# V's projection one slot later, denominators by ones in the last step but one, and products with V in parts, in a conditioned attention kernel

## The chip, the cores and the metric

One core of a Trainium2 chip runs the whole program. The metric is the time of one execution in microseconds (us). The kernel before takes 739.61 us, the median of three runs (739.45 to 740.35). Engines: PE is TensorE (matrix products), with PEld its loading of weights; ACT is ScalarE, DVE is VectorE, POOL is GpSimd, SP is SyncE, which issues nearly all transfers.

## The reference

For each of 8 sequences of 512 tokens with 512 features: attention with 16 heads of 32, with the projection of one conditioning token added to Q and K, and the input added to the result.

```python
Q = _split_heads(x @ Wq.T + bq)
K = _split_heads(x @ Wk.T + bk)
V = _split_heads(x @ Wv.T + bv)
tQ = _split_heads(tokens @ Wq.T + bq)
tK = _split_heads(tokens @ Wk.T + bk)
cQ = Q + tQ
cK = K + tK
scores = jnp.einsum('bhqd,bhkd->bhqk', cQ, cK) / jnp.sqrt(jnp.float32(HEAD_DIM))
attn = jax.nn.softmax(scores, axis=-1)
out = jnp.einsum('bhqk,bhkd->bhqd', attn, V)
x = x + out.transpose(0, 2, 1, 3).reshape(B, S, D_MODEL)
```

All is fp32.

## The kernel before, in words

**Tiling.** The work is 32 steps t (`T = B * G`), one for each sequence and group of four heads: step t is sequence t // 4, group t % 4. Scores are computed twice. Once with queries on the partitions, 128 queries (`qc`) by 512 keys for each of the four heads: from these DVE takes the row maxima (`row_max`, lines 470 to 480) and ACT the denominators, as a sum that accompanies an exponential whose own output is thrown away (`denominators`, L521). And once with keys on the partitions, 128 keys (`kc`) by 512 queries: there PE first puts the negative maxima in every row (L563, a product of ones with the maxima split in three bf16 pieces), adds the scores (L566), and ACT writes the exponentials to SBUF (`exponentials`, L577). These are the moving side of the product with V (`times_v`, L582), four heads beside each other in the columns of the array. The four `kc` of a step are called its chunks; a score burst is four products, which the trace shows as eight records, since an fp32 product runs in two passes.

**Maxima.** When the four `qc` of a step have their maxima, POOL splits them (`split_max`, L535 to L538), PE transposes them (L547), and DVE or ACT copies them from PSUM (`transpose_max`, L553). The exponentials of that step need this copy.

**Projections.** Q, K and V of two groups (for V, of half a sequence) are computed by a product scheme of seven half-size products instead of eight, split in two halves, `first_products` and `other_products`; DVE puts the parts together (`plus`, L414 and L417, and L432 to L447). The blocks of combined weights are made by POOL (`combine_w`) and of combined inputs by DVE (`combine_x`).

**The loop.** For t from 0 to 28 a step has four quarters. Quarter i issues `exponentials(t, i)`, then a `row_max` of step t+1 (in the last quarter of step t+2), and then one piece of other work: a half of Q's projection, the product of step t-1 with V and its output (`weighted`), a half of K's, a half of V's. V's half in step t is number r = t % 4 of the next sequence, while Q's and K's are those of the slot before (`qk_of`, line 806). In the last quarter `transpose_max(t + 1)` is put into V's half.

**Banks.** PSUM is one tile of eight banks. `TURNS` is a table of bank orders, eight of them used in turn by the loop: entries 0 to 3 hold the quarter's exponentials, 4 to 7 its row scores, and the other work takes banks from entries 0 to 3 again, once ACT has read the exponentials. A quarter's banks must have been read by ACT and DVE before the next quarter writes them.

**Order.** The order on PE, ACT, DVE and POOL is that of the program, and each engine takes its instructions strictly in it. SP's transfers stand in the order of issue too. Waits are put in by the framework where tiles are shared.

**Prologue.** Lines 700 to 774: transposes of weights and of the first sequence, Q and K of the first two groups, then five bursts of row maxima, (0,0) to (0,3) and (1,0), each with its denominators, and between them halves of projections: Q's two, K's first, V's two.

**Outputs.** Through step 27 the product with V stays transposed: `weighted` (lines 606 to 637) makes the reciprocals of the denominators in that layout with a small product (L621), DVE turns 32x32 blocks (L632), POOL multiplies (L633) and adds the residual (L634), and four small transfers on SP store it (L637). The residual xr has three buffers; it is loaded by four small transfers and gets V's bias on POOL (L170). From step 28 on (`turned_by_vector`, line 152) another way is used: `untranspose` on PE, `divide` on DVE, `finish`, one large transfer each way (L166, L667).

**The end.** Steps 29 to 31 are written out by hand (lines 857 to 964). The projections are over, so the row maxima of step 31 are spread in half bursts over step 29 and 30 (`row_max_pair`, `row_max_pairs`), steps 28 and 29 take their product with V in two pieces, and `keep_busy` issues 22 products whose result nobody reads. Step 31 has no denominators on ACT: DVE adds exponentials (L922, L926), and products with ones (`times_ones`, L592) give the sums over the keys.

Of the kernel before, what the change touches and what calls it, by code (L numbers as in the profile page):

```python
# [17 lines left out]
def kernel(  # L18
# [65 lines left out]
        (6, 7, 2, 3, 0, 1, 4, 5),  # L84
        (7, 2, 0, 1, 3, 4, 5, 6),
        (3, 0, 1, 2, 6, 7, 4, 5),
        (6, 7, 0, 1, 4, 5, 2, 3),
        (4, 5, 0, 1, 6, 7, 2, 3),
        (6, 7, 0, 1, 4, 5, 2, 3),
        (4, 7, 0, 1, 2, 3, 5, 6),  # L90
        (0, 3, 1, 2, 6, 7, 4, 5),

        (6, 7, 4, 5, 2, 3, 0, 1),
        (6, 7, 2, 3, 0, 1, 4, 5),
        (6, 7, 0, 1, 4, 5, 2, 3),
        (6, 7, 4, 5, 2, 3, 0, 1),
        (6, 7, 2, 3, 4, 5, 0, 1),
# [52 lines left out]
    def turned_by_vector(t):  # L150

        return t < T - 4
# [317 lines left out]
    def row_max(t, qc):  # L470
        if t >= T:
            return
        open_max(t)
        for j in range(HG):
            row_scores(t, qc, j, banks(HG + j))
        for j in range(2):
            nc.vector.tensor_reduce(  # L477
                nmax[t][:, qc, j : j + 1, 0], banks(HG + j), AX.X, ALU.max, negate=True
            )
        row_max_of(t, qc, 1, banks(HG + 2, 2))  # L480
# [16 lines left out]
    def row_max_pair(t, qc, pr, at=2):  # L497

        open_max(t)
        for i in range(2):  # L500
            row_scores(t, qc, pr * 2 + i, banks(at + i))
        row_max_of(t, qc, pr, banks(at, 2))

    def row_max_pairs(t, of, late=()):

        open_max(t)
        for k, (qc, pr) in enumerate(of):
            for i in range(2):
                row_scores(t, qc, pr * 2 + i, banks(HG + k * 2 + i))
        row_max_of(t, *of[0], banks(HG, 2))  # L510
        for f in late:
            f()
        row_max_of(t, *of[1], banks(HG + 2, 2))

    def denominators(t, qc, prs=range(NP)):

        if t >= T - 1:
            return
# [71 lines left out]
    def times_ones(of, pt, start):  # L590
        for j in range(HG):
# [5 lines left out]
                stop=not start,  # L597
            )

    oT = {}  # L600

    def leave(t, pt):
        oT[t] = op.tile([P, S], F32, tag="oT", name=f"oT_{t}")
        nc.vector.tensor_copy(oT[t], pt)

    def weighted(t, pt, pd, between):


# [7 lines left out]
        )  # L616
        for kc in range(NS):
            times_v(t, kc, pt)
            if kc == 0:
                for h in range(HG):  # L620
                    nc.tensor.matmul(  # L621
                        pd[h * BL : (h + 1) * BL, : NB],
                        modulo,
                        apart[:, h].rearrange("p c a -> p (c a)"),
                        start=True,
                        stop=True,
                    )
        rec = op.tile([P, NB, 1], F32, tag="recs", name=f"recs_{t}")
        nc.vector.reciprocal(rec, pd[:, :NB].unsqueeze(2))
        between()  # L630
        y = op.tile([P, NB, BL], F32, tag="res", name=f"res_{t}")
        nc.vector.transpose(y.rearrange("p f e -> p (f e)"), pt)  # L632
# [11 lines left out]

    res = {}

    recs = {}

    def invert(t, den):
        recs[t] = op.tile([P, NS, HG, 1], F32, tag="rec", name=f"rec_{t}")  # L650
        nc.vector.reciprocal(recs[t], den)

    def divide(t, pt):
        res[t] = op.tile([P, NS, P], F32, tag="res", name=f"res_{t}")
        nc.vector.tensor_tensor(
            res[t].rearrange("p c (h e) -> p c h e", h=HG),
            pt.rearrange("p (c h e) -> p c h e", c=NS, h=HG),
            recs[t].broadcast_to([P, NS, HG, HD]),
            ALU.mult,
        )  # L660

    def finish(t):
        b, g = divmod(t, G)
        y = res.pop(t)
# [331 lines left out]
```

## Time and profile before

| What | Value |
|---|---|
| median of three runs | 739.61 us |
| the profiled execution: its own time | 740.33 us |
| its span, first to last instruction | 737.5 us |
| PE busy | 729.1 us |
| ACT busy | 626.4 us |
| DVE busy | 529.9 us |
| POOL busy | 166.2 us |
| L521, exponentials for the denominators | 496 of 701 ns, and 496 reads of the sum of 219 ns |
| L577, exponentials kept | 512 of 603 ns |
| L493, maxima of two heads | 132 of 1214 ns |
| additions of 128x512 on POOL (L634) | 28 of 1273 ns |
| large residual loads, issue to landing | 3.8 us |

The execution is inside the span by 2.8 us, which belong to the launch and its end. A row such as "L521 ... x496 | 338.0, 701" says: 496 instructions of line 521, 338.0 us busy in total, 701 ns on average. In a timeline a row has its start, its length, the engine, the line, the operation and its tiles; the brackets say how long the engine had been idle and what ended that.

### The profile page before, as it was taken

What the parts mean: (1) busy time and instruction counts of PE and PEld (TensorE: products, weight loads), DVE (VectorE), ACT (ScalarE), POOL (GpSimd) and SP (SyncE); (2) the same over time, 40 slices, a digit from 0 to 9 for tenths busy, and PEclk for the clock granted to TensorE, in tenths of its full rate; (3) what the DMA queues carried; (4) which work ended last, traced back from release to release, by engine and by line L of the source; (5) the groups of instructions that cost most, each with busy time, mean ns of one, the idle gap of its engine ahead of it and who ended that gap; (6) DMA issues with size and microseconds to landing.
All of it is one profiled execution on the core that took longest, in us unless ns stands there. A gap on an engine that the chain in (4) does not pass through costs nothing.

```text
span 737.5 us, 15136 instructions
## 1 busy us (share of the span) xinstructions
PE 729.1 (99%) x5434; PEld 406.9 (55%) x5434; DVE 529.9 (72%) x851; ACT 626.4 (85%) x1567; POOL 166.2 (23%) x270
## 2 busy tenths in 40 slices
PE   9999999999999999999999999999999999999997
PEld 6576555655555665555565555565555555555432
DVE  3589677777677776787866877777767777667764
ACT  2569889888898988988988988988989898898965
POOL 3721211222211222211122221122221122221130
PEclk9999999999999999999999999999999999999999
DMA  8512212122212222212222221212110111110111
GB/s 263 84 20 39 35 25 44 30 44 44 38 25 40 38 35 44 44 26 34 42 31 44 44 32 27 44 30 44 30 26 9 26 30 29 30 29 12 33 30 29
DMA packets 184766, 29.63 MB, mean 40 GB/s; under 512 B 178410, under 2 KB 182506, under 8 KB 184692
## 3 DMA queue, kind: packets, MB, share of 16 engines
q1 hardware_dynamic: 184112, 28.01, 22.1%
q8 instruction: 42, 0.69, 0.4%
q10 hardware_dynamic: 580, 0.68, 0.3%
q14 instruction: 32, 0.26, 0.1%
HBM read 20.27 MB, written 8.39 MB: 39 GB/s over the span
## 4 chain that ended last, share of the span: by engine, by line
PE 97%; DVE 1%; ACT 1%; DMA 0%; issue 0%; DVEq 0%
PE psum L394 26%; PE psum L582 16%; PE psum L484 15%; PE psum L566 15%; PE psum L391 14%; PE psum L563 6%; PE psum L338 2%; PE psum L547 1%; ACT e L577 1%; PE psum L254 1%; DMA x<-in_x_dram 0%; PE psum L299 0%; PE psum L641 0%; DVE nmax L477 0%; PE psum L592 0%; PE psum L680 0%
## 5 line engine op out<-in xcount | busy, mean ns | idle before, releaser
L521 ACT ACTIVATE dead<-psum,nmax 128x512 f32<-128x512 f32 x496 | 338.0, 701 | 8.3 <-DVE nmax L477 5.4
L577 ACT ACTIVATE e<-psum 128x512 f32<-128x512 f32 x512 | 264.3, 603 | 73.0 <-PE psum L566 72.9
L477 DVE TENSOR_REDUCE nmax<-psum 128x1 f32<-128x512 f32 x248 | 159.7, 686 | 149.5 <-PE psum L484 149.5
L493 DVE TENSOR_REDUCE nmax<-psum 128x2 f32<-128x1024 f32 x132 | 160.2, 1214 | 2.8 <-PE psum L484 2.8
L484 PE MATMUL psum<-kT,qT 32*128 32x512 f32 x1024 | 140.3, 602 | 0.2 <-DVE kT L417 0.2
L566 PE MATMUL psum<-qT,kT 32*128 32x512 f32 x1024 | 132.6, 588 | 0.0
L633 POOL TENSOR_TENSOR res<-res,recs 128x512 f32<-128x512 f32 x28 | 29.3, 1047 | 436.9 <-DVE res L632 436.9
L582 PE MATMUL psum<-e,v 128*32 128x512 f32 x1024 | 120.3, 596 | 1.0 <-ACT e L577 0.9
L521 ACT ACTIVATION_READ_ACCUMULATOR dead<-psum,nmax 128x1 f32 x496 | 108.6, 219 | 0.0
L484 PEld LDWEIGHTS psum<-kT,qT 32*128 32x128 f32 x1024 | 56.7, 183 | 61.0 <-ACT dead L521 26.8
L582 PEld LDWEIGHTS psum<-e,v 128*32 128x32 f32 x1024 | 26.8, 110 | 65.9 <-issue 41.1
L563 PE MATMUL psum<-maxT,onesb 3*128 3x512 bf16 x512 | 51.4, 384 | 1.5 <-DVE maxT L553 0.8
L566 PEld LDWEIGHTS psum<-qT,kT 32*128 32x128 f32 x1024 | 51.2, 185 | 2.5 <-issue 0.2
L391 PE MATMUL psum<-wc_v,xc 128*128 128x256 f32 x192 | 49.3, 379 | 0.0
L563 PEld LDWEIGHTS <-onesb 3*128 3x128 bf16 x512 | 13.3, 91 | 60.4 <-issue 50.9
L394 PE MATMUL psum<-xc,wc_q 128*128 128x256 f32 x180 | 46.2, 379 | 0.0
L394 PE MATMUL psum<-xc,wc_k 128*128 128x256 f32 x180 | 46.2, 379 | 0.0
L391 PEld LDWEIGHTS psum<-wc_v,xc 128*128 128x128 f32 x192 | 36.5, 190 | 5.0
L391 PE MATMUL psum<-wT_v,xT 128*128 128x256 f32 x128 | 38.7, 404 | 0.0
L394 PEld LDWEIGHTS psum<-xc,wc_q 128*128 128x128 f32 x180 | 34.2, 190 | 4.7
L394 PEld LDWEIGHTS psum<-xc,wc_k 128*128 128x128 f32 x180 | 34.2, 190 | 4.7
L634 POOL TENSOR_TENSOR res<-res,xr 128x512 f32<-128x512 f32 x28 | 35.7, 1273 | 2.2
(158 smaller groups left out, 776.2 us busy)
## 6 DMA issues: line engine op xcount, KB each, us to landing
x<-in_x_dram SPq DMA_DIRECT2D x112, 64.0 KB, 2.4
xr<-in_x_dram SPq DMA_DIRECT2D x112, 64.0 KB, 2.5
out_dram<-res SPq DMA_DIRECT2D x112, 64.0 KB, 2.0
w_q<-in_L_cond_Wq_dram SPq DMA_DIRECT2D x4, 256.0 KB, 4.5
w_k<-in_L_cond_Wk_dram SPq DMA_DIRECT2D x4, 256.0 KB, 4.3
w_v<-in_L_cond_Wv_dram SPq DMA_DIRECT2D x4, 256.0 KB, 5.1
xr<-in_x_dram SPq DMA_DIRECT2D x4, 256.0 KB, 3.8
out_dram<-res SPq DMA_DIRECT2D x3, 256.0 KB, 2.4
```

What stands on the lines that cost most here:

```text
L391: nc.tensor.matmul(pt, xb, w, start=(kc == kcs[0]), stop=(kc == kcs[-1]))
L394: nc.tensor.matmul(pt, w, xb, start=(kc == kcs[0]), stop=(kc == kcs[-1]))
L477: nc.vector.tensor_reduce(nmax[t][:, qc, j : j + 1, 0], banks(HG + j), AX.X, ALU.max, negate=True)
L484: nc.tensor.matmul(pt, qkT["q", t][r, qc * P : (qc + 1) * P], qkT["k", t][r, :], start=True, stop=True,)
L493: nc.vector.tensor_reduce(nmax[t][:, qc, pr * 2 : pr * 2 + 2, 0], pt, AX.X, ALU.max, negate=True)
L521: nc.scalar.activation(dead, banks(HG + j), AF.Exp, bias=nmax[t][:, qc, j, :], accum_out=sums[t][:, qc, j, :],)
L563: nc.tensor.matmul(bank[j], onesb[r, :], maxT[t][r, :], start=True, stop=False)
L566: nc.tensor.matmul(bank[j], qkT["k", t][r, kc * P : (kc + 1) * P], qkT["q", t][r, :], start=False, stop=True,)
L577: nc.scalar.activation(e[:, i, :], bank[pr * 2 + i], AF.Exp)
L582: nc.tensor.matmul(pt[j * HD : (j + 1) * HD, :], vs[b % 2][:, kc, (g * HG + j) * HD : (g * HG + j + 1) * HD], es[t, kc, j // 2][:, j % 2, ...
L633: nc.gpsimd.tensor_tensor(y, y, rec.broadcast_to([P, NB, BL]), ALU.mult)
L634: nc.gpsimd.tensor_tensor(y, y, xr.pop(t), ALU.add)
```

## The change

V's halves in the loop are now those of the same slot as Q's and K's, so one half leaves the prologue (where K's second half takes the place of V's), V of the first sequence is made during step 0, and step 28 still has one. All entries of `TURNS` for the loop and the three last steps are new; the five of the prologue are the same.

Step 30 has no denominators on ACT either; it gets them as step 31 does, by sums of exponentials on DVE and POOL and products with ones. The row maxima of steps 30 and 31 are taken in full bursts of four heads, in two instructions of two heads on DVE, to the last quarter of step 30, and the fillers are gone. Through step 30 the output goes the transposed way with small transfers. The products with V of steps 28 to 30 are made in parts of one or two chunks: ACT copies each part from PSUM and POOL adds it to the ones before.

```diff
@@ turned_by_vector / row_max / denominators @@
-        return t < T - 4
+        return t < T - 1
...
+        if t < T - 2:
+            for j in range(2):
+                nc.vector.tensor_reduce(
+                    nmax[t][:, qc, j : j + 1, 0], banks(HG + j), AX.X, ALU.max, negate=True
+                )
+        else:
+            row_max_of(t, qc, 0, banks(HG, 2))
         row_max_of(t, qc, 1, banks(HG + 2, 2))
...
-        if t >= T - 1:
+        if t >= T - 2:
             return
@@ prologue @@
     other_products("q", 0, 1, lambda: denominators(0, 2), nothing, (0, 1))
-    first_products("k", 0, 1, nothing, nothing, 3, 2)
     advance()
     row_max(0, 3)
     split_max(0)
-    first_products("v", 0, 0, lambda: denominators(0, 3), nothing, 2, 3)
+    first_products("k", 0, 1, lambda: denominators(0, 3), nothing, 2, 3)
...
-    other_products("v", 0, 0, lambda: denominators(1, 0), nothing, (0, 2))
+    other_products("k", 0, 1, lambda: denominators(1, 0), nothing, (0, 2))
@@ loop @@
-            other_products("k", 0, 1, dens, nothing, (0, 3))
+            first_products("v", 0, 0, dens, nothing, 3)
...
-            first_products("v", 0, 1, dens, nothing, 1)
-            combine_x(1, 0)
+            dens()
+            other_products("v", 0, 0, nothing, nothing, (1, 0))
...
-            other_products("v", 0, 1, dens, nothing, (0, 3))
+            first_products("v", 0, 1, dens, nothing, 3)
+            combine_x(1, 0)
...
-        project_pair("v", b + 1, r, dens, small, (0, 2) if r % 2 else 1)
+        project_pair("v", *of, dens, small, 1 if r % 2 else (0, 2))
@@ the parts @@
+    def part_of(t, pt, of, between=None):
+
+        for k, kc in enumerate(of):
+            if k and between:
+                between()
+            times_v(t, kc, pt, of)
+        if t in parts:
+            p = op.tile([P, S], F32, tag="dead", name=f"part_{t}_{of[0]}")
+            nc.scalar.copy(p, pt)
+            nc.gpsimd.tensor_tensor(parts[t], parts[t], p, ALU.add)
+        else:
...
+            nc.scalar.copy(parts[t], pt)
...
+    def send_parts(t, den):
+        rec = op.tile([P, NB, 1], F32, tag="recs", name=f"recs_{t}")
+        nc.vector.reciprocal(rec, den)
+        send(t, parts[t], rec)
@@ steps 29 to 31 @@
+    t = T - 3
...
+    row(3)
+    exponentials(t, 3)
+    row_max(t + 2, 0)
+    part_of(t, banks(0), [0, 1], lambda: transpose_max(t + 1, banks(1), nc.scalar.copy))
+    send_parts(t - 1, den)
+
+    t = T - 2
+    row(0)
+    exponentials(t, 0)
+    row_max(t + 1, 1)
+    apart = masked(t - 1)
+    part_of(t - 1, banks(0), [2])
+    load_residual(t + 1)
+    row(1)
+    exponentials(t, 1)
+    row_max(t + 1, 2)
+    part_of(t - 1, banks(0), [3])
+    spread_sums(apart, banks(1))
+    den = denominators_of(t - 1, banks(1))
+    row(2)
+    exponentials(t, 2)
+    row_max(t + 1, 3)
+    acc = room_for_sums(t)
+    sum_of(t, acc, 1, nc.gpsimd, [0])
+    split_max(t + 1)
+    part_of(t, banks(0), [0])
+    send_parts(t - 1, den)
+
+    exponentials(t, 3, (1, 2, 3, 4))
+    sum_of(t, acc, 1, nc.vector, [1])
+    part_of(
+        t, bank(5), [1, 2], lambda: transpose_max(t + 1, bank(0), nc.vector.tensor_copy)
+    )
+    sum_of(t, acc, 2, nc.vector)
+    sum_of(t, acc, 3, nc.vector)
+
+    t = T - 1
+    exponentials(t, 0, (6, 7, 1, 2))
+    part_of(t - 1, bank(3), [3])
+    exponentials(t, 1, (0, 4, 5, 6))
+    pv = bank(7)
+    times_v(t, 0, pv)
+    exponentials(t, 2, (1, 2, 3, 0))
+    times_v(t, 1, pv)
+    times_ones(acc, bank(4), True, True)
...
+    sum_of(t, acc2, 1, nc.vector)
...
+    send_parts(t - 1, den[:, :, 0:1])
+    exponentials(t, 3, (5, 6, 1, 2))
+    times_v(t, 2, pv)
+    pd = bank(3)
+    times_ones(acc2, pd, True, False)
+    times_ones([es[t, 2, pr] for pr in range(NP)], pd, False, False)
+    times_ones([es[t, 3, pr] for pr in range(NP)], pd, False, True)
+    times_v(t, 3, pv)
```

`sum_of(t, to, kc, on, prs)` adds exponentials of chunk `kc` to the sums, for pairs of heads `prs`, on the engine `on`; `room_for_sums` takes a tile for them; `masked`, `spread_sums` and `send` are pieces of the old `weighted`; `row(i)` sets the bank order. The loop's bank orders:

```diff
-        (6, 7, 2, 3, 0, 1, 4, 5),
-        (7, 2, 0, 1, 3, 4, 5, 6),
-        (3, 0, 1, 2, 6, 7, 4, 5),
-        (6, 7, 0, 1, 4, 5, 2, 3),
-        (4, 5, 0, 1, 6, 7, 2, 3),
-        (6, 7, 0, 1, 4, 5, 2, 3),
-        (4, 7, 0, 1, 2, 3, 5, 6),
-        (0, 3, 1, 2, 6, 7, 4, 5),
...
+        (3, 0, 1, 2, 4, 5, 6, 7),
+        (4, 5, 0, 1, 2, 3, 6, 7),
+        (2, 5, 0, 1, 3, 4, 6, 7),
+        (0, 5, 3, 4, 6, 7, 1, 2),
+        (6, 7, 4, 5, 0, 1, 2, 3),
+        (4, 5, 0, 1, 2, 3, 6, 7),
+        (2, 5, 0, 1, 6, 7, 3, 4),
+        (6, 7, 0, 1, 2, 3, 4, 5),
```

## The prediction

> **What bounds the kernel now.** First the totals of the page and its chain of work that ended last, then the busy times by stretch, then the timeline of a quarter of the loop with a store and the load behind it, of the prologue, and of the end.
>
> ```profile
> span 737.5 us, 15136 instructions
> PE 729.1 (99%) x5434; PEld 406.9 (55%) x5434; DVE 529.9 (72%) x851; ACT 626.4 (85%) x1567; POOL 166.2 (23%) x270
> ...
> PE 97%; DVE 1%; ACT 1%; DMA 0%; issue 0%; DVEq 0%
> ```
>
> TensorE carries 97% of the chain. A busy PE row hides short waits, so I read its pace from the starts of its bursts. By stretch:
>
> ```profile
> core 0: us, PE busy (x) PEld busy (x) DVE busy (x) ACT busy (x) POOL busy (x), PEclk, DMA share, GB/s
> 500.00:600.00 100.00, 100.00 (x756) 56.69 (x752) 74.74 (x121) 89.48 (x227) 23.88 (x40) 1.00 0.18 28
> 680.00:690.00 10.00, 9.13 (x76) 3.81 (x78) 6.62 (x10) 9.52 (x26) 2.19 (x5) 1.00 0.28 55
> 690.00:700.00 10.00, 9.31 (x94) 5.21 (x90) 8.05 (x11) 9.14 (x25) 1.27 (x1) 1.00 0.05 12
> 700.00:710.00 10.00, 9.01 (x80) 3.35 (x72) 7.30 (x9) 7.22 (x18) 3.41 (x6) 1.00 0.15 42
> ```
>
> In the loop PE never rests; from 680 us, where the projections have ended, ACT is the fuller engine (9.52 of 10 us) and PE waits. The timeline of one quarter of the loop (in step 28), in which step 27's output leaves:
>
> ```profile
> 676.25 0.39 PE L563 MATMUL psum<-maxT,onesb 3*128 3x512 bf16 x4
> 677.24 1.05 POOL L633 TENSOR_TENSOR res<-res,recs 128x512 f32<-128x512 f32 x1 [15.56 <-DVE res L632]
> 677.34 1.02 PE L484 MATMUL psum<-kT,qT 32*128 32x512 f32 x8
> 677.53 2.06 ACT L577 ACTIVATE e<-psum 128x512 f32<-128x512 f32 x4 [0.86 <-PE psum L566]
> 678.36 1.27 POOL L634 TENSOR_TENSOR res<-res,xr 128x512 f32<-128x512 f32 x1
> 678.39 1.29 DVE L477 TENSOR_REDUCE nmax<-psum 128x1 f32<-128x512 f32 x2 [1.23 <-PE psum L484]
> 679.59 1.21 DVE L493 TENSOR_REDUCE nmax<-psum 128x2 f32<-128x1024 f32 x1
> 679.66 1.94 SPq L637 DMA_DIRECT2D out_dram<-res  x4
> 681.51 0.39 PE L563 MATMUL psum<-maxT,onesb 3*128 3x512 bf16 x4
> 681.65 0.51 SPq L166 DMA_DIRECT2D xr<-in_x_dram  x1
> ```
>
> Read as prices from a quarter's start (its L563 burst): score burst for the maxima at +1.09; first maxima 1.05 to 1.09 after that burst starts; exponentials on ACT from +1.29 to +3.35; half a projection 3.22 (the chain's commonest piece); one chunk of e times V 0.87, 1.0 alone. From POOL's L633 to the issue of the next residual load on SP pass 4.41 us, for that load stands behind four stores.
>
> **Part 1, V's half projections one slot later.** In the loop each step issues the same instructions, and V's halves issue no DMA and keep the place of the x loads. Only two ends change. The prologue loses one half: -3.22. Against it, with the new bank order, stand waits, each from the release and need in the timeline. Row maxima (0,3) now follow (0,2) without 3.1 us of K between: their bank is freed by the L521 ending at 41.18, needed at 40.4: +0.8. The first exponentials need the last L521 of row (1,0) (52.78 against 52.14): +0.6. In step 0, V's first halves use the exponentials' fourth bank, freed at +3.40, needed at +2.97: twice 0.4; V's other half uses their second (+2.42 against +2.05): 0.3; next quarter's exponentials wait for it: 0.2. Sum: -3.22 + 2.7 = -0.5; I take -0.3, since a late bank also stretches its burst by some 0.1; ends -2 (half of these waits covered) and +0.5. At the other end step 28's last quarter becomes a full V quarter: 5.64 instead of 5.26, +0.4.
>
> **The bank order of the loop.** I laid each quarter's releases against the next one's needs. Before, the quarters take 5.27, 5.68, 5.27, 5.63, 5.26, 5.76, 5.27, 5.65 over two steps; three hold about 0.09 each, where a row bank comes free over 1.0 us into the quarter (L521 ending at 649.64 for the quarter begun at 648.62). After, the same three kinds meet a late bank, only at another place in the burst; a fourth gets a bank at +0.99. Ends: -0.19 (both odd quarters cured) and +0.08 per two steps, times 14: -2.6 and +1.1. I take +0.1: nearest is the order before, same releases.
>
> **Part 2, steps 29 to 31.** Gone from ACT: step 30's 16 L521 (pitch 0.66 us, 10.6 us), which held PE from 682 to 703. Gone from PE: 22 filler matmuls and 12 transposes (2 us each by rows). Added: PE two bursts of ones (0.87 each) and two small sums (0.3 each); ACT nine copies of about 0.6 and two small; DVE three more sums of 1.22, where PE waits for none of them; POOL six part additions (1.27) and one 128x1024 sum, not in the trace: its 128x256 and 128x512 additions take 0.72 and 1.27, so about 2.4. ACT's copies wait for PE's chunk with the next exponentials behind them; that is in the replay below. SP: twelve small stores and twelve small loads in place of three large ones each, on which only the wait below hangs; the last two residual loads move (step 30's two quarters earlier, step 31's one later).
>
> I replayed the quarters with these prices, counting from A, the first exponentials of step 29. Step 29 starts its quarters at 0, 4.0, 7.4, 10.9. Two chunks fill the first (1.09 + 1.06 + 1.85); the next two are held by DVE: 1.09 + 1.09 + 1.21 = 3.4, because a bank of the maxima is needed by the next exponentials. Step 30: 15.4, 18.7, 22.3, 25.8. Now the wait that decides. Step 31's split maxima are POOL work behind a queue. DVE turns step 28's sums at 16.0 to 16.7; POOL divides and adds until 19.1; SP's four stores follow, then step 31's residual load at 21.1 (the 4.41 above), in step 28's buffer. It lands 3.8 later (median of 256 KB loads; seen 2.9 and 4.7): 24.9. All that time POOL stands at the bias addition (L170). Behind it are: bias 1.25, a part addition 1.25, the 2.4 us sum, the split 1.23: 31.0. The maxima themselves are done at 27.0, so without the queue the split ends at 28.3; PE finished all else at 27.8. So PE waits 3.3 us, then transposes, multiplies a chunk, and step 31's exponentials start at 32.4, not 29.7. Step 31 is ACT's pace: 32.4, 34.5, 36.9, 39.9, and after the last quarter's five bursts PE ends at 45.4.
>
> Before, the same stretch:
>
> ```profile
> 686.77 0.39 PE L563 MATMUL psum<-maxT,onesb 3*128 3x512 bf16 x4
> ...
> 706.94 0.40 PE L563 MATMUL psum<-maxT,onesb 3*128 3x512 bf16 x4 [0.85 <-DVE maxT L553]
> ...
> 718.88 0.60 PE L563 MATMUL psum<-maxT,onesb 3*128 3x512 bf16 x4
> ...
> 731.81 0.66 PE L641 MATMUL psum<-ident,den 128*128 128x128 f32 x4
> ```
>
> That is 731.88 - 686.77 = 45.1 to PE's last product, and 5.6 from there to the end, which the same final instructions keep; step 30's late store is issued at about 46.3 and is covered by them. So the tail gives 45.4 - 45.1 = +0.3, with V's +0.4: +0.7. The 10.6 us taken from ACT bring 20.2 - 15.4 = 4.8 us in step 29; step 30, 11.9 us before, takes 17.0, because it now holds three full bursts of step 31's maxima (five of eight half bursts had been worked off in step 29 before) and the wait.
>
> **POOL beside DVE, and a rule against it.** DVE's 1.22 us sum of step 30 falls beside POOL's 2.4 us sum. The trace's POOL additions of 128x512 take 1262 to 1281 ns throughout. Bounds: 0 if the two do not disturb each other, 1.2 if POOL stands still meanwhile; I take 0.3, near the undisturbed rows. The Trainium skill, "GPSIMD Engine Reference", section Specifications, says that GpSimd shares its SBUF interfaces with VectorE and contends with DVE instructions that read two SBUF inputs. By that rule it would be the upper end and the total nearer 741.3; by the rows, which show no slow addition, 740.1.
>
> **Sum.** -0.3 + 0.1 + 0.7 + 0.3 = +0.8 on the profiled execution's span of 737.5 (its own time 740.33, 2.8 around the span and 0.7 above the median of the runs). Carried to the median: 739.61 + 0.8 = 740.4. About 0.2%, 1.5 us, is what a measurement of this kernel tells from no change, so this is no change, leaning slower.
>
> **Rivals.**
> Slower: PE's clock falls in the 3.3 us wait. For it: this PE gap is four times any late one before (0.7 to 0.9). Against: the granted clock is 1.00 in every stretch, 0.99 in the last. If the first three bursts after the wait (0.95 + 1.1 + 0.95) took twice as long: +3.0, 743.4; it decides from a wait about as long as this. "TensorE: Matmul & The Clock Gate", section What's actually happening, has the clock halved after an idle window of about 3.4 us; no stretch here shows it, and by that rule 3.3 us just escapes.
> Faster, the loop: both odd quarters lose their late bank: -2.6, so 737.7. For: the bank orders are all new. Against: the releases come equally late and all four banks must be written.
> Faster, the tail: POOL's wait does not reach PE, if the residual lands 2.7 us earlier: 740.4 - 2.7 = 737.7. Against: the shortest landing seen is 0.9 less than the median, which gives 739.5.
> V's half staying where ACT or DMA hides it is no case: the order of PE's instructions has moved.
>
> **How the numbers follow.** Likeliest case 0.48, own range 739.2 to 741.9 (landing 0.9 either way, loop up to +1.1, contention up to 1.2): 0.33 in it is within 0.2%, 0.15 slower. Clock falls: 0.20, slower. Loop relieved: 0.15, of it 0.11 faster. Tail free: 0.11, of it 0.08 faster. More waits in the front or the loop than I found: 0.06, of it 0.05 slower. Faster 0.19, within 0.2% 0.41, slower 0.40. The range 737.7 to 743.6 reaches both faster ends and the clock's price.
>
> **What would show it.** Right: prologue's first L563 burst near 50.5 us and step 1 starting within 0.5 us of 73.6; loop 43.8 per two steps; POOL idle before the last residual's bias addition for about 4 us, a PE gap of about 3 us before step 31's transposed maxima, at full clock; 45.4 from step 29's first burst to PE's last product. Wrong: no such gap, a clock under 0.95 after it, or a loop whose two steps differ from 43.8 by over 0.1.

## The result, and the profile after

The changed kernel takes 742.62 us, the median of six runs (741.48 to 744.17), beside 739.62 for the kernel before (six runs, 739.21 to 740.36): a ratio of 1.004, 95% interval 1.0026 to 1.0054. It is slower, by twice what a measurement of this kernel can tell. A later group on another chip gave 742.15 (five runs, 741.45 to 743.23) and 1.0037 (1.0024 to 1.0049). The forecast of 740.4 was too low by 2.2 us; the time lies inside the stated 737.7 to 743.6, but outside the likeliest case's own range of 739.2 to 741.9.

The profiled execution, with a span of 739.6 and its own time of 741.48, is nearly the fastest of the eleven. In spans the two profiled executions differ by 2.1 us; in own times by 1.15, since 2.8 us lie around the span of before and 1.9 around this one. Totals and chain by engine, from its page:

```profile
span 739.6 us, 15126 instructions
PE 729.2 (99%) x5432; PEld 406.5 (55%) x5432; DVE 535.2 (72%) x845; ACT 620.6 (84%) x1546; POOL 185.3 (25%) x283
...
PE 94%; POOL 1%; DVE 1%; ACT 1%; DMA 1%; issue 1%; SPq 0%; DVEq 0%; POOLq 0%; ACTq 0%
```

POOL and DMA have come into the chain. Busy times by stretch (after the colon: the stretch's length, then PE, PEld, DVE, ACT, POOL, the granted clock, the DMA share, GB/s):

```profile
500.00:600.00 100.00, 100.00 (x756) 57.16 (x750) 75.01 (x120) 89.15 (x226) 23.89 (x40) 1.00 0.18 28
680.00:690.00 10.00, 10.00 (x76) 5.58 (x78) 7.34 (x11) 5.99 (x14) 3.46 (x6) 1.00 0.35 55
690.00:700.00 10.00, 10.00 (x96) 3.35 (x92) 5.96 (x6) 7.12 (x16) 2.49 (x7) 1.00 0.00 0
700.00:710.00 10.00, 10.00 (x96) 3.28 (x90) 7.52 (x8) 7.32 (x15) 5.06 (x6) 1.00 0.26 50
710.00:720.00 10.00, 7.13 (x66) 2.00 (x60) 7.13 (x9) 5.30 (x10) 8.87 (x9) 1.00 0.02 5
```

The loop is as it was. From 680 to 710 us PE no longer waits and ACT is down from 9.52 to 5.99 us in the first stretch: that part of the change does what it says. From 710 to 720 PE works 7.13 us, where before it worked all 10:

```profile
710.00:720.00 10.00, 10.00 (x88) 3.23 (x84) 4.59 (x7) 6.43 (x13) 2.20 (x5) 1.00 0.10 28
```

The timeline of the changed kernel from there to the end (start, length, engine and line; in brackets the idle time before and its releaser):

```profile
705.63 1.95 SPq L627 DMA_DIRECT2D out_dram<-res  x4
707.62 0.51 SPq L165 DMA_DIRECT2D xr<-in_x_dram  x1
710.83 1.28 POOL L169 TENSOR_TENSOR xr<-xr,bvb 128x512 f32<-128x512 f32 x1 [3.48 <-DMA xr<-in_x_dram]
712.07 1.27 POOL L751 TENSOR_TENSOR parts<-parts,part 128x512 f32<-128x512 f32 x1
713.29 2.37 POOL L824 TENSOR_TENSOR acc<-e,e 128x1024 f32<-128x1024 f32 x1
714.52 2.22 DVE L824 TENSOR_TENSOR acc<-e,e 128x1024 f32<-128x1024 f32 x1
715.59 1.26 POOL L519 CAST split<-nmax 128x16 bf16<-128x16 f32 x1
717.56 0.27 POOL L522 TENSOR_TENSOR split<-rest,split 128x16 bf16<-128x16 f32 x1
717.88 0.40 PE L531 MATMUL psum<-identb,split 128*128 128x128 bf16 x4 [2.87 <-POOL split L522]
718.73 7.87 DVE L826 TENSOR_TENSOR acc<-acc,e 128x1024 f32<-128x1024 f32 x4
718.87 2.20 POOL L624 TENSOR_TENSOR res<-res,xr 128x512 f32<-128x512 f32 x1
719.21 0.39 PE L547 MATMUL psum<-maxT,onesb 3*128 3x512 bf16 x4
721.04 4.48 POOL L751 TENSOR_TENSOR parts<-parts,part 128x512 f32<-128x512 f32 x2
725.65 2.05 PE L576 MATMUL psum<-acc,ones 128*32 128x512 f32 x8
727.64 0.40 PE L547 MATMUL psum<-maxT,onesb 3*128 3x512 bf16 x4
733.30 0.66 PE L631 MATMUL psum<-ident,den 128*128 128x128 f32 x4
734.86 0.76 DVE L931 TENSOR_TENSOR res<-psum,rec 128x256 f32<-128x256 f32 x2 [0.54 <-PE psum L928]
```

The reader is to see three things. First, the wait that the prediction named: POOL stands 3.48 us for step 31's residual, which SP issues behind four stores; behind POOL's bias addition stand a part addition, a sum and the split, and PE stands 2.87 us before the transposed maxima. Secondly, rows that are longer than their like: a sum on DVE takes 2.22 instead of 1.22 us, four take 7.87 instead of 4.9, an addition of 128x512 on POOL 2.20 instead of 1.27, and a conversion of 128x16 1.26 instead of 0.25; each of them has a row of the other engine beside it. Thirdly, the end: from PE's L631 to the end of the span 6.30 us, where before it was 5.69.

### The profile page after: what moved, and what is told of

It is laid out like the page before. It is cut to its first block, busy times and chain, and to the rows that moved or that the text cites. A ratio compares the mean times of both kernels' runs of the same rounds, so it can differ in the third digit from the quotient of the medians.

```text
span 739.6 us, 15126 instructions
## 1 busy us (share of the span) xinstructions
PE 729.2 (99%) x5432; PEld 406.5 (55%) x5432; DVE 535.2 (72%) x845; ACT 620.6 (84%) x1546; POOL 185.3 (25%) x283
## 4 chain that ended last, share of the span: by engine, by line
PE 94%; POOL 1%; DVE 1%; ACT 1%; DMA 1%; issue 1%; SPq 0%; DVEq 0%; POOLq 0%; ACTq 0%
PE psum L393 25%; PE psum L566 15%; PE psum L486 15%; PE psum L550 14%; PE psum L390 14%; PE psum L547 6%; PE psum L337 2%; PE psum L531 1%; DVE nmax L495 1%; PE psum L253 1%; ACT e L561 1%; PE psum L576 1%; DMA x<-in_x_dram 1%; DMA xr<-in_x_dram 0%; PE psum L298 0%
## 5 line engine op out<-in xcount | busy, mean ns | idle before, releaser
L505 ACT ACTIVATE dead<-psum,nmax 128x512 f32<-128x512 f32 x480 | 326.9, 700 | 8.1 <-DVE nmax L477 5.4
L477 DVE TENSOR_REDUCE nmax<-psum 128x1 f32<-128x512 f32 x240 | 154.7, 686 | 144.6 <-PE psum L486 144.6
L495 DVE TENSOR_REDUCE nmax<-psum 128x2 f32<-128x1024 f32 x136 | 164.7, 1216 | 10.4 <-PE psum L486 9.1
L623 POOL TENSOR_TENSOR res<-res,recs 128x512 f32<-128x512 f32 x31 | 32.4, 1047 | 443.5 <-DVE res L622 443.5
L486 PE MATMUL psum<-kT,qT 32*128 32x512 f32 x1024 | 137.2, 601 | 0.1
L505 ACT ACTIVATION_READ_ACCUMULATOR dead<-psum,nmax 128x1 f32 x480 | 104.6, 218 | 0.0
L486 PEld LDWEIGHTS psum<-kT,qT 32*128 32x128 f32 x1024 | 58.3, 183 | 57.0 <-ACT dead L505 20.6
L624 POOL TENSOR_TENSOR res<-res,xr 128x512 f32<-128x512 f32 x31 | 40.4, 1303 | 2.4
L169 POOL TENSOR_TENSOR xr<-xr,bvs 128x512 f32<-128x512 f32 x31 | 39.3, 1268 | 2.8 <-DMA xr<-in_x_dram 2.6
```

Source lines behind the costliest of these rows:

```text
L169: nc.gpsimd.tensor_tensor(xr[t], xr[t], bias, ALU.add)
L477: nc.vector.tensor_reduce(nmax[t][:, qc, j : j + 1, 0], banks(HG + j), AX.X, ALU.max, negate=True)
L486: nc.tensor.matmul(pt, qkT["q", t][r, qc * P : (qc + 1) * P], qkT["k", t][r, :], start=True, stop=True,)
L495: nc.vector.tensor_reduce(nmax[t][:, qc, pr * 2 : pr * 2 + 2, 0], pt, AX.X, ALU.max, negate=True)
L505: nc.scalar.activation(dead, banks(HG + j), AF.Exp, bias=nmax[t][:, qc, j, :], accum_out=sums[t][:, qc, j, :],)
L624: nc.gpsimd.tensor_tensor(y, y, xr.pop(t), ALU.add)
```

## The experiments

Each kernel's median stands beside runs of the kernel before on the same chip; ratios are to those. "A" is the start of step 29's first exponentials, 686.73 in the changed kernel.

### Load step 31's residual a step earlier (e1_load_early)

```diff
-            xr[t] = op.tile([P, NS, P], F32, tag="xr", name=f"xr_{t}", bufs=3)
+            xr[t] = op.tile([P, NS, P], F32, tag="xr", name=f"xr_{t}", bufs=4)
...
     part_of(t - 1, banks(0), [0, 1])
     load_residual(t + 1)
+    load_residual(t + 2)
...
     part_of(t - 1, banks(0), [2])
-    load_residual(t + 1)
```

(The other residual tile of that tag has four buffers too.)

> The residual of step 31 gets a fourth buffer and is loaded one step earlier (behind step 30's load in step 29's first quarter), so POOL no longer stands at its bias addition behind step 28's stores. Theory (the wait for the residual sets PE's gap): the bias addition is over before step 28's division; step 31's split ends about 28.3 us after step 29's first exponentials instead of 30.8, PE's gap of 2.9 us before the transposed maxima falls under 0.7, step 31's first exponentials stand at 29.7 to 30.5 instead of 32.5, and the time falls by 2 to 2.8, to 739.8 to 740.6 us. Rival (POOL and VectorE disturb each other): the split and the part addition slow down at their new place, the sums of VectorE still take about 2 us each, and less than 1 us is gained. Rival (the clock): as the theory, and besides the spread of the runs, 2.7 us in the changed kernel, falls to about 1 us.

739.46 us (739.33 to 739.68), ratio 1.0003 (0.9995 to 1.0012): one load moved, with a buffer for it, and the slowdown is gone. The timeline:

```profile
713.82 0.26 POOL L519 CAST split<-nmax 128x16 bf16<-128x16 f32 x1 [0.61 <-DVE nmax L495]
714.46 1.26 POOL L521 CAST split<-rest 128x16 bf16<-128x16 f32 x1
716.12 0.40 PE L531 MATMUL psum<-identb,split 128*128 128x128 bf16 x4 [1.21 <-POOL split L522]
716.96 7.87 DVE L826 TENSOR_TENSOR acc<-acc,e 128x1024 f32<-128x1024 f32 x4
```

The split now waits only for the maxima, but its third instruction takes 1.26 us beside DVE's sum, so PE's gap is 1.21 us and not under 0.7; step 31's first exponentials stand at A + 30.81, 1.67 less. The span falls by 1.8 (739.6 to 737.8). The median falls by 2.7 to 3.2 (2.5 to 2.7 by the ratios), and the spread from 2.7 to 0.35 us: more went than the wait's length. That the rest is the clock the next runs show. The four sums still take 7.87 us.

### Fill the gap (e2_fill_wait)

```diff
+    def fill_and_turn():
+        for _ in range(56):
+            nc.tensor.matmul(bank(0)[:, :P], onesb, onesb, start=True, stop=True)
+        transpose_max(t + 1, bank(0), nc.vector.tensor_copy)
+
-    part_of(
-        t, bank(5), [1, 2], lambda: transpose_max(t + 1, bank(0), nc.vector.tensor_copy)
-    )
+    part_of(t, bank(5), [1, 2], fill_and_turn)
```

> 56 small products that nobody reads fill PE's gap before step 31's transposed maxima; all else is as in the changed kernel. Rival (PE's clock falls after the gap in some executions): the median falls by about 1 us, to 741.5, the mean granted clock is 0.998 or more in every run and the spread of the runs falls under 1.2 us. Theory (the gap costs only its own length): no change, 742.0 to 743.0 us, with the same spread of clocks as before the edit.

741.59 us (741.37 to 741.80), ratio 1.003 (1.0018 to 1.0042). Step 31's first exponentials stand at A + 32.67, as late as without the filling, but no execution has a lower clock any more. The intervals of the ratios overlap, so I look at single executions. The changed kernel had eleven, in two groups (on two other chips):

| mean granted clock | executions | times (us) |
|---|---|---|
| 0.998 | 3 | 741.45, 741.48, 741.73 |
| 0.995 to 0.997 | 8 | 741.99, 742.10, 742.15, 742.35, 743.15, 743.23, 743.36, 744.17 |

With the gap filled, six of six have 0.998 or more, and none is above 741.80. A mean of 0.997 alone says little, since it also holds the fall of the clock at the program's end (0.90 from 730 to 735 us in e8_late_send, where two executions have 0.997 at 738.23 and 738.31, among its fastest); in the changed kernel the times part in the same way as the clocks.

### The changed kernel again (after_again)

> The changed kernel as it stands, beside the other two of this group on the same chip. If a PE gap of 2.9 us lowers the clock in some executions only: a median of 742.2 to 743.4 us, a spread of 1.5 us or more, and in the profiled execution either full clock after the gap and a span near 739.6, or half the clock for 3.4 us and a span 0.8 to 2.5 longer. If the clock has no part in it: a spread under 1 us round one value.

742.15 us, with a spread of 1.8, and this time the profiled execution (742.35, span 740.5) is one of those with a lower clock. Its timeline and its stretches:

```profile
717.90 0.49 PE L531 MATMUL psum<-identb,split 128*128 128x128 bf16 x4 [2.85 <-POOL split L522]
718.32 1.94 PE L566 MATMUL psum<-e,v 128*32 128x512 f32 x8
```

```profile
716.00:718.00 2.00, 0.10 (x2) 0.11 (x3) 0.75 (x1) 0.04 (x1) 1.78 (x5) 1.00 0.00 0
718.00:720.00 2.00, 2.00 (x12) 0.33 (x11) 1.50 (x3) 0.00 (x0) 1.92 (x2) 0.52 0.00 0
720.00:722.00 2.00, 2.00 (x18) 0.68 (x15) 2.00 (x2) 0.59 (x1) 2.00 (x2) 0.63 0.03 8
```

The same gap, 2.85 us, and behind it a granted clock of 0.52 and 0.63; a chunk of e times V takes 1.94 instead of 1.07 us. From step 30's last exponentials to step 31's first it takes 7.76 instead of 6.81 us, the next quarter 2.80 instead of 2.18; the last one takes 3.30 instead of 4.05, because the sums have caught up meanwhile. Together 0.8 us more, and the span is 0.9 longer.

### A longer gap (e6_longer_wait)

```diff
     sum_of(t, acc, 1, nc.gpsimd, [0])
+    slow = op.tile([P, S], F32, tag="dead", name="slow")
+    for _ in range(2):
+        nc.gpsimd.tensor_tensor(slow, x31, x31, ALU.add)
     split_max(t + 1)
```

(`x31` stands for step 31's residual.)

> Two more additions of 128x512 on GpSimd ahead of step 31's split, whose result nobody reads, so that PE's gap before the transposed maxima grows from 2.9 to 5.0 to 6.0 us; all else is as in the changed kernel. If a gap costs its length alone: the changed kernel's undisturbed time of 741.5 and 2.1 to 3.1 on it, 743.6 to 744.6, at full clock after it. If a gap lowers PE's clock, and the longer the surer: every execution loses 1.0 to 1.8 us more, 744.6 to 746.4, and the records show about half the clock for some 3.4 us from the gap's end or from within it, with a spread of the runs under 1 us.

744.69 us (744.46 to 745.13), all four executions at a clock of 0.994 to 0.996. The gap is 4.94 us, 2.07 longer; without a lower clock that would give 741.5 + 2.1 = 743.6, and the fastest of the four is 0.9 above it. So the case of the falling clock holds, its size at the low end. The profiled execution:

```profile
720.12 0.48 PE L531 MATMUL psum<-identb,split 128*128 128x128 bf16 x4 [4.94 <-POOL split L522]
```

```profile
720.00:722.00 2.00, 1.88 (x12) 0.43 (x12) 1.30 (x2) 0.00 (x0) 1.92 (x3) 0.57 0.00 0
722.00:724.00 2.00, 2.00 (x16) 0.66 (x12) 2.00 (x2) 0.59 (x1) 2.00 (x2) 0.57 0.03 8
```

### The first sum on VectorE (e4_sum_on_vector)

```diff
-    sum_of(t, acc, 1, nc.gpsimd, [0])
...
-    sum_of(t, acc, 1, nc.vector, [1])
+    sum_of(t, acc, 1, nc.vector)
```

> The first sum of step 30's exponentials goes from GpSimd to VectorE (both halves there), so POOL has only bias, part addition and split behind the residual's landing. Theory (the queue on POOL sets the split): the split comes 2.4 to 3.4 us earlier, PE's gap falls from 2.9 to about 0.3, and the time falls by 2 to 2.9, to 739.7 to 740.6 us. Rival (the two engines disturb each other, so work moved from one to the other is paid twice): VectorE's five sums take 2 us each beside POOL's work, PE's product of ones with the sums waits longer than the 0.9 us of now, and less than 1 us is gained.

740.65 us (740.05 to 741.02), ratio 1.0018 (1.0009 to 1.0027). The split starts 1.66 us earlier counted from A, but PE's gap falls only to 2.01:

```profile
714.24 2.32 DVE L824 TENSOR_TENSOR acc<-e,e 128x1024 f32<-128x1024 f32 x2
714.28 1.26 POOL L521 CAST split<-rest 128x16 bf16<-128x16 f32 x1
715.63 1.06 POOL L522 TENSOR_TENSOR split<-rest,split 128x16 bf16<-128x16 f32 x1
716.75 0.61 PE L531 MATMUL psum<-identb,split 128*128 128x128 bf16 x4 [2.01 <-POOL split L522]
```

DVE now runs two sums there, and each holds up one of POOL's small instructions: work moved from one engine to the other came back as waiting, as the rival said, though at the split and not at the product of ones, which no longer waits (the last quarter takes 3.31). The gain of 1.5 to 2.0 us (1.4 to 1.6 by the ratios) lies between the two. In this profiled execution too the clock is half, for 3.4 us from 716.6 on, after a gap of only 2.01 us.

### GpSimd quiet beside the sums (e5_quiet_pool)

```diff
-        nc.gpsimd.tensor_tensor(y, y, rec.broadcast_to([P, NB, BL]), ALU.mult)
-        nc.gpsimd.tensor_tensor(y, y, xr.pop(t), ALU.add)
+        if t != T - 3:
+            nc.gpsimd.tensor_tensor(y, y, rec.broadcast_to([P, NB, BL]), ALU.mult)
+            nc.gpsimd.tensor_tensor(y, y, xr.pop(t), ALU.add)
...
-            nc.gpsimd.tensor_tensor(parts[t], parts[t], p, ALU.add)
+            if t < T - 2:
+                nc.gpsimd.tensor_tensor(parts[t], parts[t], p, ALU.add)
```

> Leaves out, on GpSimd, the multiplication and residual addition of step 29's output and the part additions of step 30 (these two steps' outputs are not the reference's); all else is as in the changed kernel. Theory (VectorE and GpSimd take turns when both add from SBUF): VectorE's four sums of step 30 return from 7.9 us to 4.9 together, PE's wait of 0.9 us before the product of ones is gone, step 31's last quarter falls from 4.05 to 3.0 to 3.2 us, and the time falls by 1 us, to 740.5 to 741.6. PE's gap before the transposed maxima stays at 2.5 us or more. Rival (the quarter is long because PE has one burst more in it): the quarter stays at 4.0 and the time within 0.4 us of 742.0.

738.85 us (738.68 to 739.31), ratio 0.9991 (0.9982 to 1.0), less than either theory said, because the edit did two things. (The kernel leaves out work that the outputs of steps 29 and 30 need, so its time prices a wait and is not that of a finished kernel.) With step 29's residual unread, its buffer was free early and step 31's residual was loaded early too: PE's gap is 1.21 us, as in e1_load_early, against what I expected. So e1_load_early, alike up to step 31's first exponentials (A + 30.81 in both), is the run to compare it with:

```profile
716.87 4.62 DVE L828 TENSOR_TENSOR acc<-acc,e 128x1024 f32<-128x1024 f32 x4
721.73 0.39 PE L547 MATMUL psum<-maxT,onesb 3*128 3x512 bf16 x4
725.03 0.40 PE L547 MATMUL psum<-maxT,onesb 3*128 3x512 bf16 x4
```

The four sums take 4.62 us instead of 7.87, no one waits for them, and the last quarter is 3.30 instead of 4.05. Taking turns costs 3 us on DVE, of which 0.75 reach PE; the medians differ by 0.6 us, the ratios by 0.0012, which is 0.9 us.

### V's move undone alone (e3_v_early)

The prologue, the loop and the loop's bank orders are those of the kernel before; the end is the changed one.

> V's move is undone alone: prologue, loop and their bank orders are those of the kernel before, and the hand-written end is the changed one. Theory (V's later place saves 3.2 us in the prologue, gives 3.1 back there in waits for banks, and makes step 28's last quarter a full one): the loop stays at 43.8 per two steps, step 1 starts within 0.3 us of 73.6, step 28's last quarter falls from 5.63 to 3.4 to 4.0, as only two chunks of e times V fill it, and the time falls by 1.4 to 2, to 740.6 to 741.2 us. Rival (the new bank order is worth something in the loop): the two-step period rises by over 0.05, and the time stays at 742 or more.

743.71 us (741.08 to 746.32), ratio 1.0062 (1.0045 to 1.0079): both theories missed. The loop keeps 43.8 per two steps. The end of step 28 does not gain:

```profile
684.25 2.35 DVE L495 TENSOR_REDUCE nmax<-psum 128x2 f32<-128x1024 f32 x2 [1.39 <-PE psum L486]
684.85 0.39 PE L531 MATMUL psum<-identb,split 128*128 128x128 bf16 x4 [0.71 <-ACT e L561]
686.52 0.41 DVE L537 COPY maxT<-psum 128x512 bf16<-128x512 bf16 x1
686.98 0.40 PE L547 MATMUL psum<-maxT,onesb 3*128 3x512 bf16 x4 [1.75 <-DVE maxT L537]
```

My sentence that two chunks of e times V would fill that quarter was wrong of this kernel: they stand in step 29, and the quarter has nothing but scores and maxima. The copy of step 29's maxima stands on DVE behind two reductions, PE is idle for 0.71 and 1.75 us, and the quarter takes 5.03. The granted clock is half from 687.8 to 691.3. So this kernel has two gaps that can lower the clock, and a mean clock down to 0.991 in its slowest execution. It says little of V's move; e10_v_early is the clean form.

### The sum behind the copy, parts added from PSUM (e7_in_turn)

To e1_load_early:

```diff
-            p = op.tile([P, S], F32, tag="dead", name=f"part_{t}_{of[0]}")
-            nc.scalar.copy(p, pt)
-            nc.gpsimd.tensor_tensor(parts[t], parts[t], p, ALU.add)
+            if t == T - 2:
+                nc.vector.tensor_tensor(parts[t], pt, parts[t], ALU.add)
+            else:
...
-    sum_of(t, acc, 1, nc.vector, [1])
...
+    def turn_and_sum():
+        transpose_max(t + 1, bank(0), nc.vector.tensor_copy)
+        sum_of(t, acc, 1, nc.vector, [1])
+
+    part_of(t, bank(5), [1, 2], turn_and_sum)
     sum_of(t, acc, 2, nc.vector)
-    sum_of(t, acc, 3, nc.vector)
...
     part_of(t - 1, bank(3), [3])
+    sum_of(t - 1, acc, 3, nc.vector)
```

The sums of chunk 3 also move, behind the last part, which the expectation does not name.

> The early residual load of before, and two edits more: VectorE's first sum of step 30 stands behind the copy of the transposed maxima instead of ahead of it, and step 30's later parts are added by VectorE straight from PSUM instead of a copy on ScalarE and an addition on GpSimd. Theory (the two engines take turns in SBUF): step 31's split is undisturbed and ends 1.0 to 1.2 us earlier, PE's gap of 1.2 us falls under 0.3; only one of GpSimd's additions still stands against the sums, so the quarter of 4.05 falls to 3.2 to 3.6; the time falls by 1.5 to 2 against the early load alone (739.46), to 737.5 to 738.0 us. Rival (VectorE's own chain is the bound): the gap goes, but PE waits for the sums by as much more, and the time stays at 738.8 to 739.5.

738.28 us (738.02 to 738.74), ratio 0.9983 (0.9975 to 0.9992): faster than the kernel before, by 0.2%. Of the expected 1.5 to 2 us it brought 1.2 by the medians, 1.5 by the ratios:

```profile
714.34 0.26 POOL L521 CAST split<-rest 128x16 bf16<-128x16 f32 x1
715.00 0.40 PE L531 MATMUL psum<-identb,split 128*128 128x128 bf16 x4 [0.21 <-POOL split L522]
716.00 2.21 POOL L624 TENSOR_TENSOR res<-res,xr 128x512 f32<-128x512 f32 x1
717.58 2.84 DVE L829 TENSOR_TENSOR acc<-acc,e 128x1024 f32<-128x1024 f32 x2
```

Undisturbed, the small instruction takes 0.26 us and the gap is 0.21. One addition of POOL still stands against the sums; the last quarter takes 3.62, at the upper end.

### Step 29's output later (e8_late_send), the last stores elsewhere (e9_stores_on_scalar)

To e7_in_turn, and then to e8_late_send:

```diff
-    send_parts(t - 1, den)
+    den29 = den
...
     sum_of(t, acc2, 1, nc.vector)
+    send_parts(t - 2, den29)
...
-    y = op.tile([P, NS, P], F32, tag="res", name="res")
+    y = op.tile([P, NS, P], F32, tag="resl", name="res", bufs=1)
```

```diff
-        (nc.sync, nc.scalar)[i].dma_start(
+        nc.scalar.dma_start(
```

> The kernel with the first sum behind the copy and parts added from PSUM, and in it step 29's output is divided and sent only after step 31's sums, so that no addition of GpSimd stands against VectorE's five sums of step 30; and the last step's result has a buffer of its own, so that its first multiplication waits for no store. Theory (taking turns): all sums take 1.2 us, the product of ones waits no more, the last quarter takes 3.0 to 3.2 us, the first multiplication of the end follows PE by 0.2 instead of 0.54 us; 0.4 to 1.2 us less than with step 29's output at its old place, 736.6 to 737.6 us. Rival (the work that was moved is in the way at the end): step 31's sums or the last stores come later by what was moved, 2 us, and the time is the same or longer.

> The late send of step 29's output with one edit more: both stores of the last step are issued by ScalarE, so that the first no longer stands behind step 30's four stores on SP. Theory (the 0.8 us won by the late send was lost in SP's queue): the last issue comes 0.1 to 0.6 us earlier than SP's 733.05, and the time falls by 0.2 to 0.7, to 737.6 to 738.2 us. Rival (the end is set by the landing of the stores, not by their issue): no change, 738.2 to 738.5.

738.35 us (738.23 to 738.91), ratio 0.9985 (0.9977 to 0.9994), and 738.64 (738.45 to 738.93), 0.9988 (0.9979 to 0.9997): nothing won. Up to the end, the late send does as the theory said: the last quarter takes 3.13 and the first multiplication of the end waits 0.24 instead of 0.49. Then SP's last store, whose addition ended at 732.19, is issued only at 733.05, behind step 30's four, and the span ends 3.65 us after it; in e7_in_turn it ends 3.21 after the last issue. With both stores on ScalarE they are issued from 732.22 on, the last at 732.74, and the span ends no sooner, at 736.9 instead of 736.7. The last issue on SP in e8_late_send, and the two on ScalarE in e9_stores_on_scalar:

```profile
733.05 0.52 SPq L945 DMA_DIRECT2D out_dram<-res  x1
732.22 0.95 ACTq L945 DMA_DIRECT2D out_dram<-res  x2
```

So an earlier issue does not bring an earlier end, as the rival said. A last store took 2.5 and 2.4 us from issue to landing in these two kernels, where eight small stores had just been issued, and 1.9 in e7_in_turn. Which transfer holds up which, no run tells apart.

### V early once more (e10_v_early)

To e7_in_turn: prologue, loop and bank orders of before, and

```diff
+        if t == T - 4:
+            transpose_max(t + 1, banks(0), nc.scalar.copy)
+            part_of(t, banks(3), [0, 1])
+            break
...
-    part_of(t - 1, banks(0), [0, 1])
+    part_of(t - 1, banks(0), [2])
...
-    part_of(t - 1, banks(0), [2])
+    part_of(t - 1, banks(0), [3])
...
-    part_of(t - 1, banks(0), [3])
```

> The kernel with the first sum behind the copy and parts added from PSUM (738.28), and in it V's projection at its place of before: prologue, loop and bank orders of before, step 28's last quarter with its transposed maxima copied by ScalarE and two chunks of its product with V, the other two chunks in the first and second quarter of step 29, none in the third. Theory (V's later place costs a full quarter at the end and saves next to nothing in the prologue): 0.1 lost in the prologue, 0.4 won in step 28's last quarter, 0.3 to 0.9 won in step 29's first quarter; the time falls by 0.5 to 1.2, to 737.1 to 737.8 us. Rival (step 29 is held by VectorE and ScalarE, not by PE's chunks): the first quarter stays at 3.7 or more or the next ones grow by what it loses, and the time stays at 738.0 to 738.6.

738.42 us (738.26 to 739.39), ratio 0.9988 (0.9979 to 0.9997), beside 0.9983: no difference. From step 28's last quarter to step 30's first it takes 20.41 instead of 21.07 us, a little less than the theory's 0.7 to 1.3: 0.37 in that quarter itself, and 0.86 in step 29's first quarter, of which its next three give back 0.57, much as the rival said. But that quarter starts 0.65 later in these two executions: 0.1 by the second quarter of step 1, 0.36 in one quarter of the loop, which takes 5.99 with V early (from 111.62 us) and 5.63 with V late, the rest spread over the loop. What V's move gains in front it loses at the end.

### A buffer of its own for the last result (e12_own_buffer)

To e7_in_turn:

```diff
-    y = op.tile([P, NS, P], F32, tag="res", name="res")
+    y = op.tile([P, NS, P], F32, tag="resl", name="res", bufs=1)
```

> The kernel with the first sum behind the copy and parts added from PSUM (738.28, 0.9983 of before), and in it one edit: the last step's result has a buffer of its own, so that its first multiplication waits for no store's release; step 29's output is sent at its old place. Theory (the seven waits ahead of that multiplication cost 0.3 us at the end): it follows PE's transposes by 0.2 instead of 0.49 us, and the time falls by 0.2 to 0.4, to 737.9 to 738.1 us or 0.9979 of before. Rival (the landing of step 30's small stores sets the end): no change, 738.2 to 738.5.

737.89 us (737.70 to 738.23), ratio 0.9977 (0.9968 to 0.9986), the fastest of all:

```profile
731.65 0.80 DVE L936 TENSOR_TENSOR res<-psum,rec 128x256 f32<-128x256 f32 x2 [0.22 <-PE psum L933]
```

From PE's last small product (L631) to the end of the span it takes 6.00 us instead of 6.25, and the median span of the runs is 736.1 instead of 736.4. The intervals of the two ratios overlap, so the gain in time, 0.4 us, is as expected but near the limit of what the runs can tell.

## Why the prediction was right or wrong

| term of the sum (us) | predicted | measured in the profiled execution |
|---|---|---|
| prologue | -0.3 | -0.1 (step 1 at 73.46, before 73.58) |
| loop | +0.1 | -0.3 (step 28 at 664.89, before 665.30) |
| V in step 28's last quarter | +0.4 | +0.4 (5.63) |
| A to PE's L631, with contention | +0.6 | +1.5 (46.57, before 45.04) |
| from there to the end | 0 | +0.6 (6.30, before 5.69) |
| sum on the span | +0.8 | +2.1 |
| lower clock, at the median | 0 (rival +3.0) | some 0.7 to 1.1 |

The prediction's 731.88 for PE's last product is 731.81 in its row, so the times before are 45.04 and 5.69, not 45.1 and 5.6. Front and loop can be read from more than one execution: the eleven traces with V late start step 1 at 73.06 to 73.64 us and the three with V early at 73.45 to 73.98, so the prologue's -0.1 is inside the scatter. From step 1's second quarter to step 28's last it takes 602.1 to 602.3 us with V late and 602.7 to 602.8 with V early, so the loop did gain.

**Right.** The prologue's waits were there: its first exponentials begin at 50.19, and 0.3 us each are lost where banks are late:

```profile
50.88 0.39 PE L547 MATMUL psum<-maxT,onesb 3*128 3x512 bf16 x2 [0.30 <-ACT dead L505]
58.94 1.13 PE L390 MATMUL psum<-wT_v,xc 128*128 128x256 f32 x4 [0.31 <-ACT e L561]
```

The loop's two steps take 43.8. V's move is worth nothing in sum, which e10_v_early confirms within the noise. The wait on POOL behind SP's stores came where it was put: step 31's first exponentials at A + 32.48, predicted 32.4, and e1_load_early shows it as the cause. The hit to 0.1 us is in part luck: the residual landed 0.6 us sooner than I took, and the split lost 1.0 to a row of DVE, which I had not seen.

**Wrong: "DVE three more sums of 1.22, where PE waits for none of them", and 0.3 for POOL beside DVE.** Of the bounds 0 and 1.2 I took the one near the undisturbed rows. But the trace of before has no addition of POOL beside a sum of DVE: its 1262 to 1281 ns are rows that never met one, and prove nothing of a meeting. There were also five meetings, not one: three additions on POOL against the sums, a sum against a sum, and the split against a sum. The sums came to set step 31's last quarter (8.4 us from its first exponentials to its last ones, predicted 7.5). The Trainium skill's rule that I weighed was the better guide. The Trainium skill, "SBUF — State Buffer", section Who interferes with whom, is sharper still: it calls the ports that the two engines share an exclusive lock, and says that a DVE instruction with two SBUF inputs contends with a GpSimd instruction that reads SBUF. The trace agrees: DVE's sum that began at 714.52 ended at 716.74, 1.08 us after POOL's had ended; in the four sums 1.22 became 2.30 us beside additions that alone take 1.27, and the split's 0.25 became 1.26 beside a sum.

**Wrong: "5.6 from there to the end, which the same final instructions keep".** The instructions are the same, what they wait for is not. By the program, the last result's buffer had been released by one store before, now by four. The trace shows DVE waiting for semaphores four times at L931, once for 0.17 us, where before it waits three times, 0.05 us at most; e7_in_turn has five such waits and the buffer of its own two. That buffer brings the 6.25 us of e7_in_turn to 6.00, and 0.4 in the medians. Of the other 0.3, 0.2 lie behind the last store's issue (3.0 us from there to the end of the span before, 3.2 in e12_own_buffer); why stays open.

**Wrong as a case, right as a rival: the clock.** The likeliest case had the wait at full clock. In eight of eleven executions, by mean clock and time, the clock fell, as the rival said, and from a gap of 2.9 us, somewhat shorter than the 3.3 that it named. Its price was too high: not three bursts at half speed one behind the other, but half the clock for 3.4 us, part of which is made good while PE would have waited for the sums: 0.8 us in the execution that was profiled, against 3.0. What made another one take 744.17 was not seen.

**Wrong: the loop's +0.1, by a quarter that was missed.** Before, the quarter begun at 111.73 takes 6.01 us, its like later 5.63. With V late it is 5.63, which is most of the loop's gain. I had read the loop only where it repeats.

## What to carry to other kernels

Before work is shared between VectorE and GpSimd, look at which of its instructions read two operands from SBUF, and cost every meeting as one standing until the other has ended: even a 0.25 us conversion on the way to the next matrix product then takes 1.26. A row of the trace prices an operation only in the company in which it ran. A gap on TensorE has a second price behind it, paid in some executions and not in others, so compare spreads and mean clocks, not only one profile; and a load that stands behind stores in its queue can be issued a step earlier, for one more buffer: here that alone took the slowdown away.

## What the runs showed of the hardware

Wherever the clock fell ahead of the last products it was half for the same time: 718.07 to 721.48, 720.30 to 723.71, 716.61 to 720.03 and 687.84 to 691.25 us in four kernels (worked out from the granted clock in quarter- or half-microsecond stretches), 3.41 us each. The Trainium skill, "TensorE: Matmul & The Clock Gate", section What's actually happening, has a free-running window of 3413 ns; the length of the falls agrees with it, and a free-running window would explain why the same gap is paid for in some executions only, which no run here tests. But the page asks for an idle window of that length; here a gap of 2.01 us was enough, and PE had been busy for 0.2 to 1.5 of the 3.41 us before each fall. After the gap of 1.21 us, seen in the traces of two kernels, none of their 21 executions has a mean clock under 0.998.

VectorE's reductions, which read PSUM, took 2.36 us for two beside GpSimd's sum and without it, and the additions of a part from PSUM 0.68: of VectorE's additions, those with both operands in SBUF were the ones lengthened beside GpSimd's.
